# Four times per batch, the second half of a projection group is issued behind the last score tile of an attention unit

## The chip, the cores and the metric

One core of a Trainium2 chip runs the whole program in one launch. The metric is device time in microseconds (us), the median of three runs. Five engines work side by side, each through its own instructions in order: PE (TensorE, matmuls; its weight loads are listed apart as PEld), DVE (VectorE), ACT (ScalarE), POOL (GpSimd) and SP (SyncE, which here only issues DMAs). Matmul results go to PSUM banks, everything else lies in SBUF. The engines wait for one another through semaphores.

## The reference, cut to what matters

Four layers are applied to x (8 batches, 256 x 512) with a context of the same shape. Only the first layer is touched:

```python
# D_MODEL=256, N_HEAD=16, D_HEAD=64, L=512, columns 0..255 use weights 0, columns 256..511 weights 1
h      = Wqkv[i] @ z[:, cols_i] + Winj[i] @ u[:, cols_i]     # (3*1024, 512) per batch
q,k,v  = split(h, 3); q = q + r_w_bias
prob   = softmax(q^T k / 8)                                  # per head, 512 x 512
out    = Wo @ (prob @ v) + bo + z                            # then a layer norm over the 256 rows
```

Layers two to four (a recurrent layer, a decoder block with an MLP, a non-local block) follow and are the same before and after.

## The kernel before, in words

The first layer is `stage_l0`. Everything in it is emitted in an order written out by hand, on PE, DVE, ACT and POOL alike. The main loop `for n in range(-1, 32)` runs over 32 *attention units*: a unit is a batch and four of its heads (two pairs of heads), four units per batch. In step n the loop computes the *scores* of unit n+1 and the *values* of unit n. I number units 0 to 31, so that unit u is scored in step u-1, and u mod 4 tells its place in the batch.

**A unit's scores** come in eight tiles, 0 to 7. For each tile `scores` (L357) issues four small matmuls (L363) into a PSUM tile `sp`, of which there are two, and a DVE maximum (L368). `exp` (L371) turns the tile into exponentials on ACT (L377, two instructions with their sums), which frees the `sp` tile. `norm` (L387) forms a reciprocal on DVE (L390) and scales one half on POOL (L391); `norm2` (L394) scales the other half on ACT (L396). `turn` (L399) transposes the tile on DVE into `pt` (L403). These four trail the scores by one or two tiles: where tile 7's scores are issued, `turn` handles tile 6. `values` (L425) is a block of 128 matmuls in the program, 256 records in the trace (L432), that reads all eight transposed tiles and needs four `mm` banks.

**Projection groups** are fitted in between the tiles. One group gives q and k of a pair of heads (`qk`, pairs 0 to 7) or a quarter of v (`v`, 0 to 3), by seven products instead of eight. `group` (L311), the first half, issues products 1, 5, 2 and 6 into two PSUM banks, copies the first bank on ACT into `s15` (L315; one buffer) and makes two sums on DVE (L353 or L355, and L319) and one on POOL (L320). `group2` (L323), the second half, issues products 7, 3 and 4 into two more banks, then three sums on DVE (L355, L353) and one on POOL (L355), which reads `s15`. All these banks, those of `values` and those of the output projection `out_proj` (L450, matmuls L455) are one pool `mm` of four, used in turn.

**The order.** `Filler` (L99) holds functions by slot; `fill.until(x)` runs all that lie at or below x, by slot. A step n spans the slots 6n to 6n+6. Its end, with t = 6n, is this:

```python
step 4:  norm; fill.until(t + 4.5); norm2; scores(6); turn; fill.until(t + 4.95); exp
step 5:  norm; fill.until(t + 5.5); norm2; scores(7); turn; fill.until(t + 5.95)
next n:  exp; norm; norm2; fill.until(t + 6.5); turn; fill.until(t + 7.5); scores(0), scores(1); values
```

`put_group(at, ...)` (L509) puts the first half at `at + 0.3`, the second at `at + 1.3`, and the loads of the weights and of their stored sums 5.2 slots ahead. Where `at` mod 6 is 4, the first half is thus issued before score tile 6 and the second between tiles 6 and 7. Per batch these are four groups: `qk` 5 (in units with u mod 4 = 1), `qk` 7 (u mod 4 = 2), `v` 0 of the next batch (3) and `qk` 3 of the next batch (0). The group that follows, with both halves, stands at the head of the next step: `v` 3, `qk` 0, `qk` 2 and `v` 2 in the same sequence. In units with u mod 4 = 2 an `out_proj` piece stands on either side of that following first half; in those with 0, one stands behind each of the score tiles 6 and 7. In the first batch POOL also forms sums of the weights (`weight_sums`, `weight_sums2`, L280 to L290) which later batches load.

Of the kernel before, what the change touches and what calls it, by code (L numbers as in the profile page):

```python
# [116 lines left out]
def stage_l0(g, pools):  # L117
# [34 lines left out]
    def load_w(kind, b, i, ts=(0, 1), eng=nc.sync):  # L152

        for t in ts:
            shape = [P, 4, ST, P] if kind == "qk" else [P, 2, ST, 256]
            w = g.wpool.tile(shape, F32, tag="w", name="w" + kind)
            raw.setdefault((kind, b, i), []).append(w)
            src = I["wqk"][i, t] if kind == "qk" else I["wv"][i // 2, i % 2, t]
            if b and t and not first_use(kind, b, i):

                w, src = (x.rearrange("p (h s) k o -> p s h k o", s=2)[:, 1] if kind == "qk" else x[:, 1] for x in (w, src))
            tc.keep_in_program_order(eng.dma_start(out=w, in_=src))
# [72 lines left out]
    def first_use(kind, b, i):  # L235

        return b == (1 if (kind, i) == ("qk", 0) else 0)
# [28 lines left out]
    def load_sums(kind, b, i, n):  # L266
        t = sums_tile(kind, b, i, n)
        tc.keep_in_program_order(nc.sync.dma_start(out=t, in_=sd[kind, i][:, n]))
        if n:
            (a11, a12, _, a22), view, of = parts(kind, b, i)  # L270
            (s1, s2), (s3, s4) = map(view, combos[kind, b, i])
            combos[kind, b, i] = dict(enumerate(map(of, (a11, a12, s4, a22, s1, s2, s3)), 1))

    def weight_sums(kind, b, i):

        t = sums_tile(kind, b, i, 0)
        (a11, a12, a21, a22), view, of = parts(kind, b, i)
        s1, s2 = view(t)
        sd[kind, i] = g.dram([P, 2, 2, 512], f"s{kind}{i}")
        nc.gpsimd.tensor_tensor(s1, a21, a22, ALU.add)  # L280
        nc.gpsimd.tensor_tensor(s2, s1, a11, ALU.subtract)
        combos[kind, b, i] = view, of, (a11, a12, a21, a22, s1, s2)

    def weight_sums2(kind, b, i):

        view, of, (a11, a12, a21, a22, s1, s2) = combos.pop((kind, b, i))
        t = sums_tile(kind, b, i, 1)
        s3, s4 = view(t)
        nc.gpsimd.tensor_tensor(s3, a11, a21, ALU.subtract)  # L289
        nc.gpsimd.tensor_tensor(s4, a12, s2, ALU.subtract)  # L290
        combos[kind, b, i] = dict(enumerate(map(of, (a11, a12, s4, a22, s1, s2, s3)), 1))
# [3 lines left out]
    def products(kind, b, i, *ns):  # L295

        bank = ps.tile([P, 2, 256], F32, tag="mm", name="gp", bufs=4)
        w, a = combos[kind, b, i], acts[b]
        for out, n in zip((bank[:, 0], bank[:, 1]), ns):
            for hf in range(2):  # L300
                for k in range(ST):
                    if kind == "qk":
                        nc.tensor.matmul(  # L303
                            out[:, hf * P : (hf + 1) * P], lhsT=w[n](hf, k), rhs=a[n](hf, k),
                            start=k == 0, stop=k == ST - 1,
                        )
                    elif hf == i % 2:
                        nc.tensor.matmul(out, lhsT=a[n](hf, k), rhs=w[n](hf, k), start=k == 0, stop=k == ST - 1)
        return bank

    def group(kind, b, i):  # L311

        b1, b2 = products(kind, b, i, 1, 5), products(kind, b, i, 2, 6)
        s15 = wk.tile([P, 2, 256], F32, tag="s15", name="s15", bufs=1)
        nc.scalar.copy(s15, b1)  # L315
        out = blocks(kind, b, i)
        add(kind, i, out[0], b2[:, 0], s15[:, 0], True)
        u2 = wk.tile([P, 256], F32, tag="u2", name="u2", bufs=1)
        nc.vector.tensor_tensor(u2, b2[:, 1], s15[:, 0], ALU.add)  # L319
        nc.gpsimd.tensor_tensor(s15[:, 0], u2, s15[:, 1], ALU.add)  # L320
        groups[kind, b, i] = out, s15, u2

    def group2(kind, b, i):  # L323
        b3, b4 = products(kind, b, i, 7, 3), products(kind, b, i, 4)
        combos.pop((kind, b, i))
        out, s15, u2 = groups.pop((kind, b, i))
        x, y = s15[:, 0], out[3]
        add(kind, i, y, b3[:, 0], u2, False)
        add(kind, i, out[1], b3[:, 1], x, True)
        add(kind, i, out[2], b4[:, 0], y, False)  # L330
        add(kind, i, out[3], y, s15[:, 1], False, nc.gpsimd)
        if kind == "v":
            store_v(b, i)
# [12 lines left out]
    def add(kind, i, out, x, y, biased, eng=nc.vector):  # L346
        if kind == "qk":
            if len(out.shape) == 4:
                x, y = (t if len(t.shape) == 4 else t.rearrange("p (h l n) -> p h l n", h=2, n=16) for t in (x, y))
            else:  # L350
                x, y = (t.rearrange("p (h l) -> p h l", h=2) for t in (x, y))
        if kind == "qk" and biased:
            eng.scalar_tensor_tensor(out, x, g.pv("rwb", i), y, ALU.add, ALU.add)  # L353
        else:
            eng.tensor_tensor(out, x, y, ALU.add)  # L355
# [49 lines left out]
    def store_v(b, i):  # L405

        if i % 2 == 0:
            vd[b, i // 2] = g.dram([4, L, P], f"v{b}_{i // 2}")
        t = vs.pop((b, i))
        for j in range(2):  # L410
            at = (2 * (i % 2) + j) * P
            tc.keep_in_program_order(nc.sync.dma_start(
                out=vd[b, i // 2][:, at : at + P].rearrange("n p c -> p n c"),
                in_=t[:, j].rearrange("p (n c) -> p n c", n=4),
            ))
# [89 lines left out]
    fill = Filler()  # L505
# [3 lines left out]
    def put_group(at, *of):  # L509
        if first_use(*of):  # L510
            if of not in raw:
                fill.put(at - LEAD, lambda: load_w(*of))
            fill.put(at - 2 + 0.45, lambda: weight_sums(*of))
            fill.put(at - 1 + 0.45, lambda: weight_sums2(*of))
            fill.put(at - 0.55, store_sums)
            fill.put(at + 0.45, store_sums)
        else:
            for n in range(2):
                fill.put(at + n - LEAD, lambda n=n: load_w(*of, (n,)))
                fill.put(at + n - LEAD, lambda n=n: load_sums(*of, n))  # L520
        fill.put(at + 0.3, lambda: group(*of))
        fill.put(at + 1.3, lambda: group2(*of))

    for b in range(B):
        s = 3 * NP * b
        if b:
            fill.put(s - 16.8, lambda b=b: load_u(b))
            steps = act_sums(b)
            for at in (-14.5, -14.5, -13.5, -13.5, -13.4, -13.4, -12.8, -12.8, -12.8):
                fill.put(s + at, lambda steps=steps: next(steps))  # L530
            put_group(s - 12, "qk", b, 0)
        for i, at in enumerate((-8, -4, 0, 6)):
            put_group(s + at, "v", b, i)
        for i, at in enumerate((-10, -6, -2, 2, 4, 8, 10), 1):
            put_group(s + at, "qk", b, i)
        for un in range(NP // 2):
            fill.put(s + 6 * un - (3.4 if un else 2.4), lambda b=b, un=un: load_v(b, un))
        for n, at in enumerate((12.1, 13.1, 14.1, 15.1, 20.6, 21.6, 22.6, 23.6)):
            fill.put(s + at, lambda b=b, n=n: out_proj(b, n))
        for part, at in enumerate((6.9, 15.4)):  # L540
            fill.put(s + at, lambda part=part: load_wo(part))
        e = s + 3 * NP
        fill.put(e + 0.45, lambda b=b: norm_sum(b))
        fill.put(e + 1.6, lambda b=b: norm_mean(b))
        fill.put(e + 3.45, lambda b=b: norm_var(b))
        for k in range(ST):
            fill.put(e + (4.48, 6.48)[k], lambda b=b, k=k: norm_scale(b, k))
        fill.put(e + 6.9, lambda b=b: store(b))
# [1219 lines left out]
```

## Time and profile before

| | us |
|---|---|
| median of three runs | 3419.73 (3419.48 to 3421.73) |
| the profiled execution, its own time | 3427.37 |
| its span, first to last instruction | 3425.6 |
| PE busy in the span | 3199.6 (93%) |
| DVE, POOL, ACT busy | 2405.1, 1663.7, 1620.0 |
| first layer, time of scores and values | some 35 to 1340 of the span |
| mean granted TensorE clock | 0.97 |

Busy time is the union of an engine's instructions. The start of a row of the timeline is given from the span's start; "x8" says that eight instructions in a row were merged, and a bracket gives the idle time before them and who ended it. Each fp32 matmul of the program is two records.

### The profile page before, as it was taken

Reading aid. Unit: us, or ns where it says so; the run is one execution under the profiler, and the core shown is the slowest. Engines: PE = TensorE matmul, PEld = TensorE weight load, DVE = VectorE, ACT = ScalarE, POOL = GpSimd, SP = SyncE. Lnnn points to the kernel's source line nnn. Section 1 sums busy time; section 2 is a strip of 40 time slices with the busy share of each in tenths; the row PEclk is TensorE's granted clock in tenths of the full one; section 3 lists DMA queues with packets and bytes.
Section 4 is the critical chain, followed back from the end, with each engine's and each line's share of the span. In section 5 each row is a group of like instructions: output and inputs, shape, how many; then the busy total and the mean of one; then the engine's idle time right before and its main releaser. Section 6 shows DMA issues by size and latency. Waiting matters only on the chain. (4 is left out here: it accounts for less than half of the span.)

```text
span 3425.6 us, 68752 instructions
## 1 busy us (share of the span) xinstructions
PE 3199.6 (93%) x26496; PEld 2272.5 (66%) x26496; DVE 2405.1 (70%) x4175; ACT 1620.0 (47%) x4006; POOL 1663.7 (49%) x1776
## 2 busy tenths in 40 slices
PE   8999999999999997879999998899989997899999
PEld 6677777777776764656666655555545553789996
DVE  4666666666666664787887887677868887677771
ACT  3455555555555553224433333666656665323223
POOL 6633233333333232456656655444434444688872
PEclk9999999999999998989999999899999998999999
DMA  7666565656656541312323323266777777400002
GB/s 266 226 203 197 188 194 189 203 183 196 204 184 211 173 130 56 117 56 88 108 94 105 99 100 107 106 234 236 247 245 249 254 258 251 163 1 1 1 13 86
DMA packets 273141, 533.08 MB, mean 156 GB/s; under 512 B 25056, under 2 KB 147312, under 8 KB 268720
## 3 DMA queue, kind: packets, MB, share of 16 engines
q1 hardware_dynamic: 251616, 456.48, 41.2%
q10 hardware_dynamic: 20528, 70.39, 5.4%
q8 instruction: 211, 3.46, 0.4%
q0 software_dynamic: 672, 1.81, 0.2%
q14 instruction: 114, 0.93, 0.1%
HBM read 411.15 MB, written 117.44 MB: 154 GB/s over the span
## 5 line engine op out<-in xcount | busy, mean ns | idle before, releaser
L391 POOL TENSOR_SCALAR pe<-pe,rinv 128x512 f32<-128x512 f32 x256 | 177.0, 692 | 618.7 <-DVE rinv L390 613.5
L368 DVE TENSOR_REDUCE nmax<-sp 128x2 f32<-128x1024 f32 x256 | 308.8, 1216 | 187.0 <-PE sp L363 187.0
L933 POOL TENSOR_TENSOR rs<-a,r 128x1024 f32<-128x1024 f32 x128 | 302.6, 2379 | 253.3 <-DVE a L928 213.4
L1161 POOL TENSOR_SCALAR pe<-pe,rinv 128x256 f32<-128x256 f32 x512 | 235.3, 479 | 338.8 <-DVE rinv L1159 334.4
L377 ACT ACTIVATE pe<-sp,nmax 128x512 f32<-128x512 f32 x512 | 347.0, 683 | 11.2
L1151 ACT ACTIVATE pe<-pe,nmax 128x256 f32<-128x256 f32 x512 | 255.0, 500 | 182.1 <-DVE nmax L1142 179.0
L403 DVE STREAM_TRANSPOSE pt<-pe 128x1024 f32<-128x1024 f32 x256 | 312.6, 1231 | 24.2 <-POOL pe L391 15.3
L432 PE MATMUL av<-pt,vr 32*64 32x256 f32 x8192 | 269.0, 395 | 45.0 <-issue 34.2
L928 DVE TENSOR_TENSOR_SCAN a<-w,vb 128x1024 f32<-128x1024 f32 x128 | 287.4, 2275 | 4.8
L432 PEld LDWEIGHTS av<-pt,vr 32*64 32x64 f32 x8192 | 213.4, 138 | 112.7 <-issue 65.1
L363 PE MATMUL sp<-k,q 64*64 64x512 f32 x2048 | 265.0, 609 | 8.3 <-ACT pe L377 8.3
L373 ACT ACTIVATE nmax<-nmax 128x2 f32<-128x2 f32 x256 | 51.8, 202 | 401.0 <-DVE nmax L368 400.8
L303 PEld LDWEIGHTS gp<-t,ws 128*128 128x128 f32 x1512 | 185.6, 192 | 30.7 <-issue 12.7
L303 PE MATMUL gp<-t,ws 128*128 128x128 f32 x1512 | 203.0, 278 | 2.0 <-POOL ws L289 1.4
L396 ACT ACTIVATE pe<-pe,rinv 128x512 f32<-128x512 f32 x256 | 182.6, 729 | 41.0 <-DVE rinv L390 41.0
L924 DVE TENSOR_TENSOR vb<-vb,k 128x1020 f32<-128x1020 f32 x128 | 157.2, 1228 | 4.3
L1171 DVE STREAM_TRANSPOSE dt<-pe 128x1024 f32<-128x1024 f32 x128 | 155.6, 1216 | 4.3 <-POOL pe L1161 4.3
L902 PE MATMUL vb<-v,mconstc 32*128 32x255 f32 x1024 | 99.1, 443 | 58.1 <-DVE a L928 58.1
L1446 ACT ACTIVATE h<-h,pvec 128x256 f32<-128x256 f32 x124 | 56.0, 500 | 201.6 <-DVE h L1415 164.6
L390 DVE RECIPROCAL rinv<-ssum 128x2 f32<-128x2 f32 x256 | 41.0, 160 | 146.7 <-ACT pe L377 146.7
L1190 PE MATMUL cp<-pt,av 128*32 128x256 f32 x1024 | 94.4, 402 | 45.0 <-DMA pt<-pt 41.3
L455 PEld LDWEIGHTS op<-av_sb,wo 128*128 128x128 f32 x512 | 92.2, 190 | 55.3 <-issue 27.5
(310 smaller groups left out, 7603.1 us busy)
## 6 DMA issues: line engine op xcount, KB each, us to landing
pt<-dt ACTq DMA_DIRECT2D x128, 512.0 KB, 3.6
pt<-pt SPq DMA_DIRECT2D x512, 128.0 KB, 3.5
ws<-sqk SPq DMA_DIRECT2D x110, 512.0 KB, 5.0
wqk<-in_wqk_dram SPq DMA_DIRECT2D x70, 512.0 KB, 5.3
vr<-v SPq DMA_DIRECT2D x128, 256.0 KB, 4.6
ws<-sv SPq DMA_DIRECT2D x56, 512.0 KB, 4.8
wv<-in_wv_dram SPq DMA_DIRECT2D x36, 512.0 KB, 4.8
v<-vT SPq DMA_DIRECT2D x64, 256.0 KB, 2.6
```

What stands on the lines that cost most here:

```text
L303: nc.tensor.matmul(out[:, hf * P : (hf + 1) * P], lhsT=w[n](hf, k), rhs=a[n](hf, k), start=k == 0, stop=k == ST - 1,)
L363: nc.tensor.matmul(sp[a * 64 : (a + 1) * 64, h, :], lhsT=qs[b, 2 * un + a][r, ic], rhs=ks[b, 2 * un + a][r, :], start=True, stop=True,)
L368: nc.vector.tensor_reduce(nmax, sp, AX.X, ALU.max, negate=True)
L377: nc.scalar.activation(pe[:, h, :], sp[:, h, :], AF.Exp, bias=nmax[:, h : h + 1], scale=1.0 / DH ** 0.5, accum_out=ssum[:, h : h + 1],)
L391: nc.gpsimd.tensor_scalar(pe[:, 0, :], pe[:, 0, :], rinv[:, 0:1], 1.0, ALU.mult, ALU.mult)
L396: nc.scalar.mul(pe[:, 1, :], pe[:, 1, :], rinv[:, 1:2])
L403: nc.vector.transpose(pts[b, un][:, it], pe)
L432: nc.tensor.matmul(av[r][h * DH : (h + 1) * DH], lhsT=vr[rows_, kb, h * DH : (h + 1) * DH], rhs=pt[rows_, :, h, 32 * kb : 32 * kb + 32], s ...
L928: nc.vector.tensor_tensor_scan(a.rearrange("p n l -> p (n l)"), w4.rearrange("p n l -> p (n l)"), vb[:, 4 * n2 : 4 * n2 + 4, :].rearrange( ...
L933: nc.gpsimd.tensor_tensor(rs, a, rb, ALU.mult)
L1151: pin(nc.scalar.activation(pe[:, r, :], pe[:, r, :], AF.Exp, bias=nmax[:, r : r + 1], scale=-1.0, accum_out=ssum[:, r : r + 1],))
L1161: pin(nc.gpsimd.tensor_scalar(pe[:, r, :], pe[:, r, :], rinv[:, r : r + 1], 1.0, ALU.mult, ALU.mult))
```

## The change

`group2` of the groups with `at` mod 6 = 4 moves from slot `at + 1.3` to `at + 1.7`, behind score tile 7 and `turn` of tile 6, and ahead of the `exp` of tile 7.

```diff
         fill.put(at + 0.3, lambda: group(*of))
-        fill.put(at + 1.3, lambda: group2(*of))
+        fill.put(at + (1.7 if at % 6 == 4 else 1.3), lambda: group2(*of))
```

In the order of each engine, for one such unit:

```diff
 PE     first half, scores 6
-       second half, scores 7
+       scores 7, second half
        following group, scores 0 and 1 of the next unit
 DVE    reciprocal 6
-       three sums of the second half, maximum 7, transpose 6
+       maximum 7, transpose 6, three sums of the second half
        reciprocal 7
```

ACT's order stays as it is but for one place in the last batch, where two pieces of the next layer's start (L83, L88, L734) now come before the second half. POOL's order changes only in the first batch: there the last sum of the second half now stands behind the two weight sums L289 and L290. No instruction is added or removed. The very first of the groups (`v` 0 of batch 0) runs before any scores, so 31 groups change place against a score tile.

## The prediction

> **What bounds the kernel now.** The page first: PE is busy nearly throughout.
>
> ```profile
> PE 3199.6 (93%) x26496; PEld 2272.5 (66%) x26496; DVE 2405.1 (70%) x4175; ACT 1620.0 (47%) x4006; POOL 1663.7 (49%) x1776
> PEclk9999999999999998989999999899999998999999
> ```
>
> Then the busy time by stretch: of 1200 us of the first layer PE works 1157.54. The two short stretches are one pair of clock windows in unit 13: PE busy 1.65 of 3.40 us, and in the next 3.40 us it gets half the clock (0.50).
>
> ```profile
> 100.00:1300.00 1200.00, 1157.54 (x14013) 867.13 (x14019) 794.36 (x1231) 651.61 (x1653) 410.45 (x535) 0.99 0.60 189
> 599.20:602.60 3.40, 1.65 (x20) 0.39 (x12) 2.59 (x6) 0.78 (x2) 2.03 (x3) 1.00 0.00 0
> 602.60:606.00 3.40, 3.40 (x65) 2.64 (x69) 2.71 (x4) 1.89 (x7) 0.98 (x2) 0.50 0.63 200
> ```
>
> So a move pays only through PE's waits. The timeline of unit 13 (u mod 4 = 1) shows where they are. PE: score tile 6, the moved half, tile 7, the following group, tiles 0 and 1, and values after a wait of 1.75 us.
>
> ```profile
> 587.16 1.09 PE L363 MATMUL sp<-k,q 64*64 64x512 f32 x8
> 588.18 1.16 PE L303 MATMUL gp<-t,ws 128*128 128x128 f32 x8
> ...
> 591.05 1.09 PE L363 MATMUL sp<-k,q 64*64 64x512 f32 x8
> 592.07 1.13 PE L308 MATMUL gp<-wv,x 128*128 128x256 f32 x4
> ...
> 598.32 1.95 PE L363 MATMUL sp<-k,q 64*64 64x512 f32 x16
> 602.01 9.58 PE L432 MATMUL av<-pt,vr 32*64 32x256 f32 x256 [1.75 <-issue]
> ```
>
> The page calls that wait "issue", but DVE shows what ended it: transpose 7 runs from 600.68 to 601.91. Before it stands a serial chain: the three sums of the moved half, maximum 7, exp 7, reciprocal 7, the ACT copy to s15, two sums, transpose 7.
>
> ```profile
> 594.30 0.61 DVE L355 TENSOR_TENSOR k<-gp,u 128x256 f32<-128x256 f32 x1
> 594.75 0.46 DVE L353 SCALAR_TENSOR_TENSOR q<-gp,pvec,s 128x256 f32<-128x256 f32 x1
> 595.12 0.59 DVE L355 TENSOR_TENSOR k<-gp,k 128x256 f32<-128x256 f32 x1
> 595.62 1.22 DVE L368 TENSOR_REDUCE nmax<-sp 128x2 f32<-128x1024 f32 x1
> 596.75 1.24 DVE L403 STREAM_TRANSPOSE pt<-pe 128x1024 f32<-128x1024 f32 x1
> 598.58 0.17 DVE L390 RECIPROCAL rinv<-ssum 128x2 f32<-128x2 f32 x1 [0.60 <-ACT pe L377]
> ...
> 600.68 1.23 DVE L403 STREAM_TRANSPOSE pt<-pe 128x1024 f32<-128x1024 f32 x1
> ```
>
> Tile 7 needs the `sp` tile of tile 5, which the exp of tile 5 frees. In unit 13 that ends at 590.02, 2.86 us after tile 6 starts:
>
> ```profile
> 589.82 0.20 ACT L377 ACTIVATION_READ_ACCUMULATOR pe<-sp,nmax 128x1 f32 x1
> ```
>
> **The change, part by part.** No instruction is added; matmul time is the same. What moves is waiting: tile 7 may now come 1.02 us behind tile 6 (the pitch of a lone tile, 591.05 to 592.07) and waits for exp 5. Where PE waited for such a tile (unit 31, tile 1), it went on 0.05 us after the exp ended. Two small savings: a group pays 0.11 us more behind scores (first eight records 1.16 against 1.05), scores 0.09 behind a group.
>
> *u mod 4 = 1 (units 5 to 29, seven).* Unit 13: tile 7 at 590.07, PE idle from 588.18 (1.89 us). The moved half from 591.09, 2.87 - 0.09 = 2.78, to 593.87; the following first half 3.56 - 0.11 = 3.45, to 597.32. Its second half reuses the moved half's first bank, which the second DVE sum frees. On DVE, maximum 7 now follows reciprocal 6: 594.30 instead of 595.62; transpose 6 at 595.43; the three sums at 596.60, 597.05 and 597.42; bank free at 597.55, PE waits 0.23. Then 2.69 for the second half and 1.87 for tiles 0 and 1: PE is ready for values at 602.11. The chain: POOL's last sum starts 0.68 after the third (as in 595.12 to 595.80), 598.10, takes 0.87, and holds the s15 copy until 599.00 (before: 599.41). So transpose 7 and the sums behind it come 0.41 earlier. Values before: start at 602.01, but the first 16 records took some 0.5 more than in undelayed units (0.95 to 1.07 against 0.48), as the fourth `mm` bank was freed only at 602.89; in effect 602.50. After: 602.11. Gain 0.4, times seven: -2.7. The new wait is paid out of the old one.
>
> *u mod 4 = 3 (3 to 27, seven).* Unit 15: exp 5 ends at 669.00, 1.70 after tile 6; tile 7 at 669.05, PE idle 0.73. Moved half 670.07 to 672.77, following first half to 676.33, values ready on PE at 680.98 (4.65 later). The s15 copy goes from 678.02 to 677.45, by the same steps (sums at 675.53 to 676.20, POOL until 677.42). Values before: 680.69 plus 0.80 lost in the first 16 records, 681.49; after 680.98. -0.5 each, -3.6.
>
> *u mod 4 = 2 (6 to 26, six).* Here values waited for nothing: transpose 7 ended 2.65 us before them. Unit 14: exp 5 ends at 627.92; tile 7 at 627.97, idle 1.10. The moved half 628.99 to 631.78, out_proj 1.83 - 0.10, following half at 633.51 instead of 632.60: +0.91. Its second bank, wanted at 635.29, is the moved half's first. Transpose 6 needs POOL's part of tile 6, which ends at 633.53 (behind the act_sums of L209), so transpose 6 at 633.57, sums at 634.74 and 635.19, bank at 635.70: +0.41. Together +1.32, nothing hides it: +7.9.
>
> *u mod 4 = 0 (4 to 28).* Exp 5 ends 0.14 before tile 6 starts, an out_proj stands before tile 7, and transpose 7 has 2.40 us in hand: 0.
>
> *Units 0 to 2.* PE waits 1.13 to 1.44 us for POOL's weight sums (L289). The POOL sum moves behind them, so they come 0.87 earlier, while tile 7 costs 0.8 to 1.1 that this wait swallows. By the same sums values come 0.6 to 0.7 earlier: -2.0. *Unit 30:* maximum 7 stands behind the next layer's L741 and L744 before and after; the three sums (1.32) now lie between transpose 6 and reciprocal 7, which idled 0.60: +0.7.
>
> Order: -2.7 - 3.6 + 7.9 + 0.7 - 2.0 = +0.3 us.
>
> *The clock.* Half-speed windows of 3.41 us follow a window of the same fixed grid in which PE idles about half. Five of the seven values of u mod 4 = 1 (5, 13, 17, 25, 29) got one, each 1.7 us (values 9.73 us in units 5 and 17 against 8.05 in unit 21). The idle time moves to tile 7 and is 1.82 us of modelled idle instead of 1.76 plus the slow first records. With some 1.7 us needed inside one window, (3.41 + 1.82 - 2 x 1.7) / 3.41 = 0.54 of the grid's phases do it: 3.8 of 7, 1.2 fewer, -2.0. Bounds: none of seven (-8.5), all (+3.4).
>
> The Trainium skill, "TensorE: Matmul & The Clock Gate", section "Why this matters for your kernels", warns only of PE idle gaps over about 3 us; here 1.75 us was followed by half the clock, so the measurement decides. By the page alone none of the new waits would halve the clock, and the sum would be 6.5 us lower.
>
> *DMA.* The group weights land 18 us or more before use, so late bank and buffer release costs nothing there. In u mod 4 = 3 the store of v 0 (SP, 674.34) waits for the moved sums and goes some 2.3 us later, with the loads behind it (675.61 to 679.65), deeper into values. There PE shows "issue" gaps of 0 to 2.10 us (7.0 in these seven units) which I take for late instruction fetches beside such loads. Cost 0 to 7 x 2.1 - 7.0 = 7.7; I take +1.0, since only the tail of the loads is new there.
>
> Sum: +0.3 - 2.0 + 1.0 = -0.7. The profiled execution took 3427.37 (span 3425.6, 1.8 around it), 7.6 above the median; the difference is applied to the median, 3419.73 - 0.7 = 3419.0.
>
> **The rivals.** *The clock is spared* (faster). Idle time at tile 7 stands between dense full-size matmuls; if these count for more than the first values did, all five windows go and none comes: -2.0 becomes -8.5, with the rest 3412.5; with the DMA term at nothing 3411.5. For it: in unit 27 a values block with a gap of 2.07 us kept its clock. Against: 2.10 us in unit 11 lost it.
>
> *Values starve* (slower). In u mod 4 = 1 the wait before values may have given PE's instruction supply time; four of its seven values (5, 13, 17, 21) have no gap later on, while those of u mod 4 = 3 and 0, with little wait, have up to 2.10. If the lost wait returns as a gap of 1.5 us there (+10.5), and 0.5 in u mod 4 = 3 (+3.5 in place of +1.0), it is 3432; at 1.0 and 0.3, 3427. It decides from the point where a fetch lands after PE has run dry, visible as "issue" within L432. Against: units 10, 14, 18, 22 and 26 start values with no wait and have no gap.
>
> That tile 7 can't move as far as the program puts it is in the forecast: it moves 1.0 us in unit 13, not 2.9.
>
> **How the numbers follow.** Forecast 0.64, clock spared 0.16, starving 0.20. A measurement of this kernel tells about 0.2% (6.8 us) from no change; forecast means same, the first rival faster, the second slower. The forecast's own range is 3414 to 3425 (clock and DMA terms between their bounds, not both at one end). To leave out no more than 2 in 10 it reaches halfway into both rivals: 3411 to 3430.
>
> **What would show it.** Right: in u mod 4 = 1, 2, 3 tile 7 waits (L363 on ACT's L377) 1.9, 1.1 and 0.7 us, with units 0, 1 and 30 some 28 us more than the 8.3 of before; values' wait of 1.75 us falls under 0.4; three to four half-clock windows start at tile 7. Wrong: tile 7 without waits; transpose 7 later than before in u mod 4 = 1; "issue" in L432 well above the 34.2 us of before (which holds the old waits); PE waits of u mod 4 = 2 far from 1.3 us.

## The result, and the profile after

On one chip the kernel before took 3419.44 us (median of 20 executions, 3410.90 to 3429.37) and the changed kernel 3427.02 us (20, 3417.42 to 3438.53). The ratio is 1.0022, 95% interval 1.0013 to 1.0030, so the change costs 7.6 us (4.4 to 10.3). The forecast was 3419.0 with "same" as the likeliest outcome; the time lies inside the range, in the case called slower.

One warning before the profiles are compared. The profiled execution of after took 3418.42 us, near the bottom of its 20; that of before took 3427.37, near the top of its own. Their difference has the wrong sign. The part behind the values of unit 31, the same in every kernel, took 2082.9 to 2096.2 us in the 14 profiles of this study, so a span alone tells little here. I compare by terms, and where a term scatters by its mean over profiles that share the feature in question.

The page of after: the engines, and the two PE groups of the prediction (line, engine, operation, tile, count | busy, mean ns | idle time before them and who ended most of it).

```profile
PE 3182.6 (93%) x26496; PEld 2261.8 (66%) x26496; DVE 2402.4 (70%) x4175; ACT 1623.5 (48%) x4006; POOL 1664.3 (49%) x1776
L363 PE MATMUL sp<-k,q 64*64 64x512 f32 x2048 | 270.2, 618 | 36.0 <-ACT pe L377 32.4
L432 PE MATMUL av<-pt,vr 32*64 32x256 f32 x8192 | 249.7, 383 | 25.3 <-issue 19.2
```

The score tiles now wait 32.4 us for the exp, against 8.3 before. "issue" ahead of the values' records fell from 34.2 to 19.2 us. That is about what the waits ahead of values had made up (12.5 us in u mod 4 = 1, 1.1 in u mod 4 = 3, 1.2 in unit 30): the gaps inside the blocks are as large in sum as before, but they stand elsewhere.

PE's timeline of unit 13 (u mod 4 = 1) shows the forecast order: tile 6, a wait, tile 7, the moved half, and values with no wait ahead of them.

```profile
580.98 1.09 PE L363 MATMUL sp<-k,q 64*64 64x512 f32 x8
583.89 1.09 PE L363 MATMUL sp<-k,q 64*64 64x512 f32 x8 [1.82 <-ACT pe L377]
584.91 1.16 PE L303 MATMUL gp<-t,ws 128*128 128x128 f32 x8
...
594.13 1.95 PE L363 MATMUL sp<-k,q 64*64 64x512 f32 x16
596.01 6.14 PE L432 MATMUL av<-pt,vr 32*64 32x256 f32 x206
```

In unit 14 (u mod 4 = 2) the two forecast waits are there, 1.02 us for the exp and 0.26 us for a bank (forecast 1.10 and 0.41). Values start 18.08 us after tile 6, against 16.69 before.

```profile
618.84 1.09 PE L363 MATMUL sp<-k,q 64*64 64x512 f32 x8
620.95 1.09 PE L363 MATMUL sp<-k,q 64*64 64x512 f32 x8 [1.02 <-ACT pe L377]
...
628.68 1.13 PE L303 MATMUL gp<-u,wqk 128*128 128x128 f32 x8 [0.26 <-PE gp L303]
...
636.92 7.16 PE L432 MATMUL av<-pt,vr 32*64 32x256 f32 x256
```

Unit 15 (u mod 4 = 3) is where the account fails. Tile 7 waits 0.67 us as forecast, values start without a wait, and then PE runs dry for 2.54 us inside the values block, where before there was no gap. Before:

```profile
680.69 8.51 PE L432 MATMUL av<-pt,vr 32*64 32x256 f32 x256 [0.16 <-issue]
```

After:

```profile
661.68 1.09 PE L363 MATMUL sp<-k,q 64*64 64x512 f32 x8
663.43 1.09 PE L363 MATMUL sp<-k,q 64*64 64x512 f32 x8 [0.67 <-ACT pe L377]
...
675.41 6.70 PE L432 MATMUL av<-pt,vr 32*64 32x256 f32 x233
684.65 1.09 PE L432 MATMUL av<-pt,vr 32*64 32x256 f32 x23 [2.54 <-issue]
```

SP's queue around it: the store of v 0 (L412) and then three pairs of loads, each a weight load (L162) and its stored sums (L268). The last of before:

```profile
679.65 0.67 SPq L268 DMA_DIRECT2D ws<-sv  x1
```

The last three of after:

```profile
674.63 0.38 SPq L268 DMA_DIRECT2D ws<-sv  x1
675.10 0.38 SPq L162 DMA_DIRECT2D wv<-in_wv_dram  x1
675.53 0.74 SPq L268 DMA_DIRECT2D ws<-sv  x1
```

In this unit the store goes out 9.3 us after tile 6, 7.0 before, which is the delay that was forecast. The last load is issued 0.1 us after values start; before it was 1.0 us ahead of them. The busy time by stretch shows what that does (PE, PEld, DVE, ACT, POOL busy, then granted clock, DMA share, GB/s). First the kernel before, counted from the start of its values at 680.69, then after, from 675.41; each from 0 to 3, 3 to 6 and 6 to 10 us:

```profile
680.69:683.69 3.00, 2.99 (x76) 2.09 (x84) 3.00 (x5) 0.62 (x2) 0.88 (x1) 1.00 0.99 343
683.69:686.69 3.00, 3.00 (x123) 2.66 (x113) 0.78 (x3) 2.57 (x9) 0.80 (x2) 1.00 0.81 313
686.69:690.69 4.00, 4.00 (x92) 2.21 (x74) 0.40 (x1) 1.76 (x6) 0.58 (x1) 1.00 0.01 4
```

```profile
675.41:678.41 3.00, 3.00 (x114) 2.91 (x118) 2.49 (x3) 1.57 (x6) 0.89 (x1) 1.00 0.89 295
678.41:681.41 3.00, 3.00 (x128) 3.00 (x117) 0.33 (x2) 1.62 (x6) 1.38 (x2) 1.00 1.00 352
681.41:685.41 4.00, 1.46 (x50) 0.77 (x34) 0.00 (x0) 0.01 (x1) 0.00 (x0) 1.00 0.25 97
```

Two things differ. The DMA engines are full to 6 us into the values and not to some 5; and PE is further on: 114 records in the first 3 us instead of 76. The trace's records of the instruction queue q8 join the two. The page lists it so (packets, MB, share of the DMA engines' time), that is 211 packets of 16 KB in the whole program:

```profile
q8 instruction: 211, 3.46, 0.4%
```

In each of these blocks one packet lands 4.6 to 7.8 us after the start (in five of the seven a second one follows near the end), and where PE has run dry it goes on 1.3 to 1.5 us after the landing. For the seven units with u mod 4 = 3, counted from the start of their values:

| unit | landing before | after | gap before | after |
|---|---|---|---|---|
| 3 | 5.79 | 5.71 | 1.07 | 1.80 |
| 7 | 5.18 | 5.24 | 1.25 | 2.08 |
| 11 | 5.27 | 4.60 | 2.10 | 2.08 |
| 15 | 6.19 | 7.82 | 0 | 2.54 |
| 19 | 5.33 | 7.14 | 0.05 | 2.54 |
| 23 | 5.28 | 5.73 | 0.46 | 1.57 |
| 27 | 5.96 | 4.97 | 2.07 | 1.31 |
| sum | | | 7.00 | 13.92 |

In units 15 and 19 the landing itself is 1.6 to 1.8 us later. In the other five it moves by -1.0 to +0.5, but PE reaches record 128 of the block 3.52 us after the start and not 4.34, because the first records no longer wait for a bank. Those 0.8 us are what the forecast had booked as a gain. PE spends them waiting for the same packet. The transfer of the packet itself is not slow: it took 0.91 to 1.04 us in these units after the change, and 0.95 to 1.31 where all the loads were moved away (experiment 4). What differs is its start, 3.7 to 6.9 us into the block against 0.7 to 2.8.

Gaps of that size also cost clock. In unit 11 a window of 3.40 us with PE busy 1.32 is followed by one at half the clock:

```profile
515.60:519.00 3.40, 1.32 (x44) 1.09 (x47) 0.17 (x1) 0.90 (x4) 1.01 (x2) 0.99 0.77 295
519.00:522.40 3.40, 3.40 (x78) 3.40 (x67) 0.00 (x0) 0.00 (x0) 0.00 (x0) 0.51 0.03 6
```

### The profile page after: what moved, and what is told of

It is laid out like the page before. It is cut to its first block, busy times and chain, and to the rows that moved or that the text cites. A ratio compares the mean times of both kernels' runs of the same rounds, so it can differ in the third digit from the quotient of the medians.

```text
span 3416.6 us, 68738 instructions
## 1 busy us (share of the span) xinstructions
PE 3182.6 (93%) x26496; PEld 2261.8 (66%) x26496; DVE 2402.4 (70%) x4175; ACT 1623.5 (48%) x4006; POOL 1664.3 (49%) x1776
## 5 line engine op out<-in xcount | busy, mean ns | idle before, releaser
L363 PE MATMUL sp<-k,q 64*64 64x512 f32 x2048 | 270.2, 618 | 36.0 <-ACT pe L377 32.4
L432 PE MATMUL av<-pt,vr 32*64 32x256 f32 x8192 | 249.7, 383 | 25.3 <-issue 19.2
L432 PEld LDWEIGHTS av<-pt,vr 32*64 32x64 f32 x8192 | 204.7, 134 | 82.4 <-issue 48.5
L363 PEld LDWEIGHTS sp<-k,q 64*64 64x64 f32 x2048 | 60.0, 132 | 139.4 <-ACT pe L377 59.2
```

The lines of the kernel that those rows point to most:

```text
L363: nc.tensor.matmul(sp[a * 64 : (a + 1) * 64, h, :], lhsT=qs[b, 2 * un + a][r, ic], rhs=ks[b, 2 * un + a][r, :], start=True, stop=True,)
L432: nc.tensor.matmul(av[r][h * DH : (h + 1) * DH], lhsT=vr[rows_, kb, h * DH : (h + 1) * DH], rhs=pt[rows_, :, h, 32 * kb : 32 * kb + 32], s ...
```

## The experiments

Ratios are to the kernel before, run on the same chip beside it, with 95% intervals; 0.001 is 3.4 us. "Gaps" are PE's idle times inside the values blocks after their first records, summed over the full units of a class (seven, or six where u mod 4 = 2). Unit 29's idle time at record 8, which a DVE sum ends, is a wait for a bank and not counted.

Theory *late loads*: the moved second half of v 0 holds its store on SP, the loads behind it go later, and the instruction packet for the values lands later. Rival, *lost wait*: the gaps come whenever the wait ahead of values goes, whatever the loads do. A third reading, named *stalls alone*, puts the loss on the waits of tile 7.

**1. The qk groups alone are moved.**

```diff
-        fill.put(at + (1.7 if at % 6 == 4 else 1.3), lambda: group2(*of))
+        fill.put(at + (1.7 if at % 6 == 4 and of[0] == "qk" else 1.3), lambda: group2(*of))
```

> Only the qk groups move (slots of qk 3, 5, 7); v 0 stays between the tiles. Measured for the whole change: +7.6 us. Theory 'late loads': the move of v 0 sends its store and the weight loads behind it some 2 us later, into the values block of units with u mod 4 = 3, where PE then runs dry (gaps inside L432 of units 3 to 27: 7.0 us in the profile before, 13.9 us after). Then this kernel has gaps of about 7 us there, and the time is before + 3.9 us (waits and returns of the order alone: -2.7 + 7.9 + 0.7 - 2.0). Rival 'stalls alone': the gaps of one profile are chance, the loss is tile 7's waits; then the move of v 0 was a gain of 3.6 us, and this kernel is before + 11 us.

Measured: 1.0009 (0.9992 to 1.0026), +3 us. Gaps of u mod 4 = 3: 8.62. One of the seven units with u mod 4 = 1 had a half-clock window. The time fits late loads and not stalls alone.

**2. Only v 0 is moved** (the condition is `of[0] == "v"`).

> Only v 0 moves. 'Late loads': gaps inside L432 of units 3 to 27 of about 14 us, tile 7 waits 0.7 us in those units alone, time before + 3.3 us (-3.6 + 6.9). 'Stalls alone': gaps about 7 us, time before - 3.6 us.

Measured: 1.0016 (1.0004 to 1.0028), +5.5 us; gaps of u mod 4 = 3: 13.93. Moving v 0 alone doubles them and makes the kernel slower.

**3. All but qk 7** (the condition is `of[::2] != ("qk", 7)`).

> All of the change but qk 7. Both theories take the loss of units with u mod 4 = 2 (1.3 us in each of seven, 0.7 in unit 30) out: after - 8 us, that is before - 0.4 us. A third, that half-clock windows at tile 7 of the units with u mod 4 = 1 make the loss, leaves it at before + 7 us. Gaps inside L432 of units 3 to 27: about 14 us by 'late loads'.

Measured: 0.9988 (0.9973 to 1.0003), -4 us. Values of u mod 4 = 2 start 16.69 us after tile 6 again; gaps of u mod 4 = 3: 14.74. So qk 7 is a pure loss of some 8 us or more, as the order account says (the ratio lies 0.0034 below that of the whole change, some 12 us, though the two were not run side by side), and the gaps stay.

**4. The changed kernel with the four load pairs put behind the values' v loads.**

```diff
+    late = {("qk", 3, 1): -2.36, ("v", 2, 0): -2.35, ("v", 2, 1): -2.34, ("qk", 4, 0): -2.33}
...
+                to = late.get((*of[::2], n), at + n - LEAD - s0) + s0     # s0 = 3 * NP * batch
-                fill.put(at + n - LEAD, lambda n=n: load_w(*of, (n,)))
-                fill.put(at + n - LEAD, lambda n=n: load_sums(*of, n))
+                fill.put(to, lambda n=n: load_w(*of, (n,)))
+                fill.put(to, lambda n=n: load_sums(*of, n))
```

> The whole change, and in each later batch the loads for the second half of qk 3, for v 2 and for the first half of qk 4 are put behind load_v of the batch, so that SP issues them after the values block of the units with u mod 4 = 3. 'Late loads': gaps inside L432 of units 3 to 27 fall from 14 us to under 2, time after - 12 us or more, some 5 us under before. 'Stalls alone' : after, unchanged (before + 7.6 us).

Measured: 0.9988 (0.9976 to 1.0000), -4 us. Gaps of u mod 4 = 3: 0.00 in all seven, with values that start without a wait; the packets there land at 1.7 to 3.9 us. But the loads now crowd into the next unit: gaps of u mod 4 = 0 rise to 9.05 (1.87 in after). The loads are the cause, and they were moved and not removed. "Lost wait" alone is dead: these values have no wait and no gap.

**5. The changed kernel again.**

> The changed kernel once more, for a second profile of it and for the pairing on this chip. Both theories: 2 to 8 us above the kernel before (ratio 1.0006 to 1.0024); gaps after the first records of the values of the seven units with u mod 4 = 3 again 12 to 15 us in sum; values of u mod 4 = 1 without the wait of 1.75 us. A second profile with other half-clock windows than the first is expected by both: 1 to 3 of 7 units with u mod 4 = 1 at half clock.

Measured: 1.0023 (1.0008 to 1.0038). Gaps 13.29; two half-clock windows in u mod 4 = 1 and four in or right behind the values of u mod 4 = 3 (two in the first profile, one in that of before).

**6 and 7. The store of v 0 put behind three of the four load pairs**, in the kernel before (6) and in the changed one (7). SP then need not wait for the moved sums before it issues the loads.

```diff
-        if kind == "v":
+        if kind == "v" and i:
             store_v(b, i)
...
+        if of[0] == "v" and not of[2]:
+            fill.put(at + 3.9, lambda: store_v(*of[1:]))
```

> The kernel before, with nothing but the store of v 0 moved on SP behind the loads of qk 3 (second tensor) and v 2. Theory of the late loads (PE's instruction fetch for the values is late when weight loads are issued within some 6 us ahead of them): SP no longer waits at that store, the loads go some 5 to 8 us earlier, the gaps in the values of u mod 4 = 3 fall from 7.0 to 0 to 3 us, and the kernel is 4 to 7 us below the kernel before (ratio 0.998 to 0.9988). Rival theory (the gaps come from the lost wait of 0.2 to 1.8 us ahead of the values, not from the loads): the gaps stay near 7, ratio 1.000.

> The changed kernel with the same move of the store of v 0 on SP. Late loads: gaps in the values of u mod 4 = 3 fall from 13.9 to 0 to 3 us although the values start without a wait, and the time falls 10 to 14 us below the changed kernel, 4 to 8 us below the kernel before (ratio 0.9977 to 0.9988). Lost wait: the gaps stay at 10 or more, ratio 1.001 to 1.002.

Measured: 6: 0.9978 (0.9962 to 0.9995), -7.5 us, gaps 7.00 to 2.20. 7: 1.0002 (0.9990 to 1.0013), 7 us below the changed kernel of experiment 5, gaps 13.92 to 6.55. In both the loads go earlier and the gaps shrink, by 4.8 and 7.4 us. In 7 less than expected, though: the packet lands at 4.79 us on average against 4.60 in 6, almost the same, and yet the gaps are 4.35 us wider. That is 0.6 per unit, most of the 0.8 that PE has won. So the rival holds a part: the faster start of values comes back as a gap wherever the packet is late. Each reading alone was wrong on 7.

**8. Only qk 5 and v 0 moved, the store of v 0 behind the loads** (the condition `of[::2] in (("qk", 5), ("v", 0))`, with the edit of 7).

> Only the second halves of qk 5 (u mod 4 = 1) and v 0 (u mod 4 = 3) are moved, those of qk 7 and qk 3 stay, and the store of v 0 stands behind the loads. Late loads: without the 8 us of qk 7 and without the gaps, order -2.7 and -3.6 and about -1 in units 1 and 3, clock -3 to -5, gaps -4 to -7: 14 to 19 us below the kernel before (ratio 0.9944 to 0.9959). Lost wait: the gaps of 14 us remain, 2 to 6 us below (ratio 0.998 to 0.9995).

Measured: 0.9977 (0.9963 to 0.9991), -8 us, no better than 6. A miss: gaps of u mod 4 = 3 were 6.97 (2.20 in 6), and those of u mod 4 = 1 6.1 (2.9 in 6). These 8 us are about what the moves were to gain.

**9 and 10. Two load pairs ahead of the values, two behind.** As 8 (9) and as 6 (10), but with the store at `at + 3.0` and only the second tensor of v 2 and the first of qk 4 behind the v loads.

```diff
+    late = {("v", 2, 1): -2.34, ("qk", 4, 0): -2.33}
```

> Moved second halves of qk 5 and v 0 alone; on SP the store of v 0 behind two of the four load pairs, the other two (second tensor of v 2, first of qk 4) behind the values' v loads of the next step. Reading so far: the gap in a values block is the landing of one instruction fetch plus some 1.5 us, less the time at which PE reaches a fixed record, and the fetch is late beside the loads ahead of values. Then with only two pairs ahead of the values of u mod 4 = 3 the fetch lands at 2 to 4 us instead of 4 to 5 (as where all four pairs were behind: 1.7 to 3.9) and the gaps there fall from 7 to 0 to 2; those of u mod 4 = 0 grow from 4.4 to at most 7. Time 6 to 12 us below the kernel before (ratio 0.9965 to 0.9982). Rival (gaps come back wherever a wait goes): gaps of u mod 4 = 3 stay at 5 to 7, ratio 0.9975 to 0.9985 as with the store alone.

> Control: the same places on SP, no second half moved. Late loads: gaps in u mod 4 = 3 at 0 to 1, those of u mod 4 = 0 at 4 to 7; waits of 12.5 us ahead of the values of u mod 4 = 1 remain with 3 to 5 half-clock windows there; 3 to 8 us below the kernel before (ratio 0.9977 to 0.9991). The difference to the kernel with qk 5 and v 0 moved is then their own worth: 3 to 6 us by the order and the clock, 0 by the rival.

Measured: 9: 0.9939 (0.9921 to 0.9958), 21 us below the kernel before (five executions, 3404.83 to 3410.98). 10: 0.9967 (0.9950 to 0.9983), -11 us. Gaps of u mod 4 = 3: 0.29 and 0.46; of u mod 4 = 0: 4.69 and 4.05. Unit 15 in kernel 9, PE's timeline and the first two of the same stretches from the start of its values:

```profile
654.20 1.09 PE L363 MATMUL sp<-k,q 64*64 64x512 f32 x8
655.95 1.09 PE L363 MATMUL sp<-k,q 64*64 64x512 f32 x8 [0.67 <-ACT pe L377]
...
667.93 7.43 PE L432 MATMUL av<-pt,vr 32*64 32x256 f32 x256
```

```profile
667.93:670.93 3.00, 3.00 (x114) 2.91 (x118) 2.50 (x3) 1.56 (x6) 0.88 (x1) 1.00 0.50 151
670.93:673.93 3.00, 3.00 (x128) 3.00 (x118) 0.34 (x2) 1.63 (x6) 1.38 (x2) 1.00 0.04 8
```

The order is that of after, the pace of PE is that of after (114 and 128 records), the DMA engines are idle from the fourth microsecond on, and the block has no gap. Only now are the moves of qk 5 and v 0 worth something: 9 is 0.0028 of the ratio, some 10 us, below 10 (I expected 3 to 6). By the executions of 9 and 10 themselves, five and nine, it is 9 us, with an interval of some 5 to 12; with the loads half in the way 8 and 6 were equal.

**11 and 12. Transfers that nobody reads, put where there was never a gap.** The kernel before plus copies of 512 KB from DRAM to DRAM on SP, near the values of u mod 4 = 2: four per batch (11), three (12).

```diff
+    def extra(b, n):
+        w = g.dram([P, 4, ST, P], f"extra{b}_{n}")
+        tc.keep_in_program_order(nc.sync.dma_start(out=w, in_=I["wqk"][7, 0]))
...
+        for n, at in enumerate((12.7, 12.7, 12.9, 12.9)):      # 12: (12.9, 12.9, 12.9)
+            fill.put(s + at, lambda b=b, n=n: extra(b, n))
```

> The kernel before plus work that nobody reads: in each batch four copies of 512 KB from DRAM to DRAM on SP's queue, around the pair of loads ahead of the values of u mod 4 = 2, which have never had a gap. Late loads: the fetch in these values lands later than the usual 3.2 to 3.7 us and a gap of 0.5 to 2.5 us opens in most of the eight blocks, 4 to 16 us in sum, with no change of order and no lost wait; time up by that much (ratio 1.001 to 1.005). Lost wait: no gap there, ratio 1.000.

> The kernel before plus three copies of 512 KB from DRAM to DRAM per batch that nobody reads, now behind the pair of loads, so that they are issued from 0.7 us ahead of the values of u mod 4 = 2 and keep the DMA engines full to some 4 to 7 us into them, as the loads do in u mod 4 = 3. Late loads (the fetch waits behind what keeps the DMA engines full): the fetch that lay at 0.5 to 3.8 us goes to 3.7 us or later and gaps of 0.5 to 2.5 us open in at least four of the six full blocks, 4 to 12 us in sum; ratio 1.001 to 1.004. If gaps need a lost wait, or something in the order of u mod 4 = 3: none there, ratio 1.000.

Measured: 11: 1.0007 (0.9993 to 1.0022). Two copies went out 11.8 us ahead of the values and two 5.8 ahead, where SP had room; the DMA engines were full to some 2 us into them, and two of the six full blocks showed a gap, 1.17 us in sum. Too early to decide. 12: 1.0023 (1.0010 to 1.0037), +8 us. All three went out 5.8 us ahead, not 0.7 as I had meant, but the engines stayed full to some 4 us into the values, and a gap opened in all six blocks: 1.24, 1.00, 0.81, 0.72, 0.53 and 0.26 us, 4.56 in sum. Unit 10 in kernel 12, PE's timeline:

```profile
484.06 6.30 PE L432 MATMUL av<-pt,vr 32*64 32x256 f32 x224
491.36 1.12 PE L432 MATMUL av<-pt,vr 32*64 32x256 f32 x32 [1.00 <-issue]
```

and the stretch from 3 to 6 us into these values, in the kernel before and in 12:

```profile
482.36:485.36 3.00, 3.00 (x128) 2.63 (x117) 0.17 (x1) 0.78 (x4) 0.89 (x2) 1.00 0.03 11
```

```profile
487.06:490.06 3.00, 3.00 (x128) 2.62 (x111) 0.17 (x1) 0.79 (x4) 0.91 (x2) 1.00 0.39 141
```

PE does the same 128 records in both; what differs is the DMA share, and 0.3 us later PE runs dry. Transfers alone, with no order changed and no wait removed, make the gap. Of the 8 us of kernel 12 its gaps explain some 5; the rest is open.

## Why the prediction was wrong

Taken step by step; "first" and "second" are the two profiles of after (that of the result and that of experiment 5).

**Tile 7's waits: right.** Forecast 1.9, 1.1 and 0.7 us in units 13, 14 and 15; measured 1.82, 1.02 and 0.67. L363's wait for the exp was forecast at some 36 us and is 32.4.

**Order, u mod 4 = 1: right.** Forecast -2.7. Tile 6 to the end of values, without the gaps and the half-clock windows, is 2.2 us (first) and 2.8 us (second) shorter over the seven units.

**Order, u mod 4 = 2: right.** Forecast +7.9; +8.9 in both. This is the largest single loss, and experiment 3 shows it by itself.

**Order, u mod 4 = 3: right on paper, worth nothing.** Forecast -3.6; without the gaps and the half-clock windows the seven units are 3.6 and 3.7 us shorter. But the working treated the end of values as fixed by the start of values. In these units it is fixed by the landing of a packet plus 1.3 to 1.5 us.

**The DMA term: the step that failed.** The prediction had the mechanism (the store 2.3 us later, the loads behind it, late instruction fetches) and the bounds, 0 to 7.7. It then wrote "I take +1.0, since only the tail of the loads is new there". This is the term that was mis-sized: it measured some +6.6. The gaps grew by 6.9 and 6.3 us: to 14.0 on average in the four profiles with v 0 moved and SP's order left as it was, against 7.2 in four with v 0 in place too. The reason given was about bytes. What counts, by the landings and by experiments 4, 6, 7 and 9, is when the loads are through and the packet can start, against PE's place in the block, and the change moved both the wrong way. The rival "values starve" had just this, "0.5 in u mod 4 = 3 (+3.5 in place of +1.0)"; that part came true at twice the size. Its other part, the lost wait of u mod 4 = 1 coming back as a gap, hardly did: the rival put it at 7.0 to 10.5 us, and the gaps there average 3.1 us (0.8 to 6.1) in the eight profiles with qk 5 moved and 2.3 (0.9 to 4.4) in the six without.

**The clock: right in sign, small in size, and one part missing.** Forecast 1.2 fewer half-clock windows in u mod 4 = 1, -2.0 us. Profiles with the old wait in place show 3 to 5 of seven (mean 4.0), those with qk 5 moved 1 to 3 (mean 2.1): 1.9 fewer, -3.2 us at 1.71 each. What was missed: the long gaps of u mod 4 = 3 bring new windows. With v 0 moved and SP's order as it was there are 2 to 4 of them (mean 2.5), with v 0 and SP's order both as before 0 or 1 (mean 0.75 in four profiles), +3.0 us; the prediction had put this at nothing. The Trainium skill ("TensorE: Matmul & The Clock Gate", section "HAM oscillation — how this bites in real kernels") puts the limit at idle gaps of more than some 3.4 us; the 2.08 us of unit 11 halved the clock here, so the measurement decides again.

**Units 0 to 2 and 30: the ends.** Without gaps and clock, units 0 to 2 are 1.0 and 1.4 us shorter (forecast -2.0). Their gaps also fell, from 5.5 on average (five profiles with no group moved) to 2.0, which I did not foresee; why is open (among those five they ran from 2.6 to 6.6). In unit 30 values start 2.6 us later after tile 6 (17.32 to 19.90), but that is mostly a half-clock stretch of 6.83 us, which lay almost wholly in the values before and lies mostly ahead of them now: to the end of values the unit takes 27.64 us before, 27.81 and 27.55 after. Over all profiles it takes 27.0 to 28.2 us (mean 27.7) in the five with qk 7 moved and 24.8 to 27.6 (mean 25.7) in the nine without, where the half clock lasts one window or two: +2.0, against a forecast of +0.7.

The sum, by these means, in the order of the paragraphs: -2.5 + 8.9 - 3.6 + 6.6 - 3.2 + 3.0 - 1.2 - 3.5 + 2.0 = +6.5 us, against 7.6 measured (4.4 to 10.3). Several of the terms scatter by 2 us or more from profile to profile, so the agreement says at most that no large term is missing. Single profiles can't show the sum: from tile 6 of unit 0 to the end of the values of unit 31 they took 1286.7 us before and 1280.9 and 1288.1 after. What is shown, since an experiment switched it, is the loss at qk 7 (3), the gap at the loads (2, 4, 6, 7, 9, 10) and that transfers alone make it (12).

One of the prediction's own signs would have misled: it asked for "issue" in L432 "well above the 34.2 us of before", and the page's total fell to 19.2, because the waits that went hid the gaps that came. The classes of units have to be read apart.

## What to carry to other kernels

When a change holds up a store or a wait on the queue that also carries bulk loads, look at what PE executes while these loads drain: a block with many short matmuls uses up instructions fast, and its next packet may land late. A wait removed ahead of such a block is a gain only if the end of the block isn't set by that landing; so the loads are put right first, and the order of the work is tuned after that (the same two moves were worth nothing with the loads half in the way and some 9 us without). And a move that is good at one place of a repeating pattern isn't good at all: of the four groups here two, moved together, pay once the loads are out of the way, one loses 8 us, and one (qk 3, not tried alone) leaves the time from tile 6 to values as it was, 16.48 and 16.49 us.

## What the runs showed of the hardware that I had not expected

- PE's instructions arrive during the run, in packets of 16 KB on queue q8. While the DMA engines were full (share 0.8 to 1.0) well into a values block, the packet landed 4.6 to 7.8 us after its start; with loads moved away (experiments 4 and 9), 1.7 to 4.6. In the 14 profiles PE runs dry for over 0.15 us inside values blocks 216 times, and each time it went on 1.2 to 1.6 us after a packet had landed.
- The record at which PE runs dry is a fixed place of the program (174 in unit 3, 149 in unit 7, 124 in unit 11 of the kernel before; where these units have a gap in the other kernels, it is within four records of it, or of a place 128 records further on). So it seems that the packets' borders decide which unit suffers.
- Seven idle times of 1.82 us at tile 7 cost fewer half-clock windows (1 to 3 in eight profiles) than seven of 1.75 us ahead of values did (3 to 5 in six profiles). In each profile these windows begin on one grid of 3.413 us. Ahead of values, the clock halved behind 20 of the 24 idle times whose worst window of the grid had PE busy for under half of it, and behind 3 of the other 18. At tile 7 it halved behind 17 of the 22 with PE busy for under 0.47, and behind none of the other 34, eight of which lay between 0.47 and 0.50. So a window about half idle is what costs the clock here, and the border lies a little lower at tile 7; I have not found out what makes that difference.
